# A four-layer graph network kernel: the value weights in one load, and layer 0's other loads issued some row tiles earlier

## The chip, the cores and the metric

The kernel runs on one core of a Trainium2 chip. A core has four computing engines that run side by side, each through its own instructions in order: TensorE (PE, matrix products; PEld is its loading of the stationary operand), VectorE (DVE), ScalarE (ACT) and GpSimd (POOL). SyncE (SP) only issues transfers. Sixteen DMA engines carry the transfers of all queues. The metric is device time in microseconds (us) of one launch; smaller is better.

## The reference

There are N = 2708 nodes with 512 features each (x) and an adjacency matrix adj (2708 x 2708) of which most entries are zero. Four layers follow each other; each normalises x over the features, applies a relu, computes something with adj, and adds it to x:

```python
# layer 0
h = relu(layernorm(x)); head = adj > 0, each row divided by its norm
x = x + ((adj + head) @ h) / rowsum(adj + head)
# layer 1: attention with 8 heads of 64, masked where adj is not one or more
x = x + sum over heads of softmax(q k^T / 8 - 1e16 * (1 - max(adj, I))) @ (h Wv) @ Wo
# layer 2
g = relu(adj @ (h W1) + b1); g = relu(adj @ (g W3) + b3); x = x + tanh(g Wf + bf)
# layer 3
x = x + ((adj != 0) @ (h W + b)) / degree
```

The mask of layer 1 is so strong that, if the largest entry of a row of adj stands alone and the scores are bounded, a row attends to one node only: the one where that row is largest. The kernel computes layer 1 in this way: it finds the place of each row's maximum (two passes of DVE over a row tile), multiplies by one product of the value and output weights, and gathers rows. Flags are collected on the way (that the scores are bounded, that no entry is negative, that the maximum is alone), and if a flag is set, a slow version of the layers runs instead.

## The kernel before, in words

Rows of adj are handled in NT = 22 tiles of 128 (the last has 20). Layer 0 is the part that the change touches; it takes the first 522 us of the span.

For each row tile, a slab of adj (128 x 2708, 1.35 MB) is loaded by SP (`load_slab`, L480) into one of three buffers named `ar`. On ACT, `row_norm` (L501) takes the signs of the slab (L510) and counts them (L515), and `row_sum` sums it (L529). `attended` (L535) finds the maximum and its place on DVE (L542, L544). Counted masks of three tiles go through TensorE (`count`, L273), ranks are formed, and `search` (L369) turns them on DVE into lists of the rows and blocks that aren't empty. POOL then gathers those (`gather_adj` L562 from adj, `gather_rows` L580 from h). The product of a row tile (L778) takes six dense blocks and five to eight gathered ones (the last tile: two gathered ones alone); for the first LEAD = 3 tiles it takes all 22 blocks. After it, `xt` is formed on DVE (L787) and normalised; `after` (L714) transposes the result on TensorE (L192), copies it on ACT (`hT`, L193) and multiplies it by the weights `wvo` of layer 1 (L158), whose result `yo` is stored.

The loop over m runs one row tile of products while the statistics of a tile up to eight further on are taken (`stats_to`, L677). Slabs 0, 3, 4, 5 and 1, 2 are needed early for their counts but their signs and maxima are not taken then: the tiles in `LATE` (3, 4, 5, 0, 1, 2) are loaded a second time, and `count_signs` (L493) and `attended` run on them in the last row tiles:

```python
if m + 8 > NT and late:
    if late[0] not in slab:
        load_slab(late[0])
    if len(late) > 1:
        load_slab(late[1])
    count_signs(late[0])
    attended(late.pop(0))
```

Weights come in between. At the very start ACT's queue loads the value weights, 1 MB in eight heads with runs of 256 bytes (`load_values`, L432), and the output weights (L436). `value_weights` (L438) transposes the first on TensorE (16 transposes, L445, four rounds of four with a copy by DVE, L446, after each), and multiplies the two into `wvo` (L158, copied by ACT, L450). `score_bound` (L453) loads the query and key weights (1 MB each, L461) and squares them on ACT (L464) at row tile 15. W1, 1 MB, is loaded and split into three parts for layer 2 (`load_w` L170, `split_w` L209, four rounds of ACT L197 and L207 and DVE L199 and L204) at row tile 17; W3 is loaded after it.

The order in which each engine gets its instructions is not just that of the program: the framework's scheduler moves an instruction ahead of others on its engine if its operands are free by the scheduler's own reckoning of times. To hold a transfer to its row tile, the kernel writes one element of its destination from that tile's `xt` with a small DVE copy (`behind`, L162, recorded under L164): the transfer then has to wait for it.

Of the kernel before, what the change touches and what calls it, by code (L numbers as in the profile page):

```python
# [9 lines left out]
FP = mybir.dt.float32  # L10
# [12 lines left out]
P = 128  # L23
# [19 lines left out]
def kernel(  # L43
# [27 lines left out]
    nc = tc.nc  # L71

    N, D = x.shape
    H, _, DK = wk_d.shape
    NT = (N + P - 1) // P
    NFULL = N // P
    TAIL = N - NFULL * P
    NCD = D // P
# [83 lines left out]
    def behind(dst, last):  # L162

        nc.vector.tensor_copy(dst, last)  # L164
# [41 lines left out]
        )  # L206
        nc.scalar.activation(lo, lo.bitcast(FP), AF.Copy, scale=-SHIFT)  # L207

    def split_w(pool, raw, tag):  # L209

        w = [pool.tile([P, NCD, D], FR, name=f"{tag}{i}") for i in range(3)]
        for c in range(NCD):
            split_b(*(part[:, c, :] for part in w), raw[:, c, :])
        return w

# [8 lines left out]
    with tc.tile_pool(name="l0_slab", bufs=2) as slabs, tc.tile_pool(  # L224
# [199 lines left out]
                norm(wp, h0[t], n, h0[t], AF.Relu)  # L424
                nc.gpsimd.dma_start(out=h0d[span(t)], in_=h0[t][:n])

        wv = wset.tile([P, NCD, D], FP, name="wa0")
        wo = wset.tile([P, NCD, D], FP, name="wa1")

        def load_values():  # L430
            for h in range(H):
                nc.scalar.dma_start(  # L432
                    out=wv[:, :, h * DK : (h + 1) * DK],
                    in_=wv_d[h].rearrange("(c p) k -> p c k", p=P),
                )
            nc.scalar.dma_start(out=wo, in_=wo_d.rearrange("(c p) k -> p c k", p=P))  # L436

        def value_weights():  # L438

            wvo = hp.tile([P, NCD, D], FP, name="wvo")  # L440
            wvt = wset.tile([P, NCD, D], FP, name="wa2")
            for r in range(NCD):
                pt = ps_tr.tile([P, NCD, P], FP, name="pt")
                for c in range(NCD):
                    nc.tensor.transpose(pt[:, c, :], wv[:, c, r * P : (r + 1) * P], ident)  # L445
                nc.vector.tensor_copy(wvt[:, r, :], pt.rearrange("p c k -> p (c k)"))  # L446
            for r in range(NCD):
                acc = ps_y.tile([P, D], FP, name="yacc")
                project(acc, wvt[:, :, r * P : (r + 1) * P], P, wo)
                nc.scalar.copy(wvo[:, r, :], acc)  # L450
            return wvo

        def score_bound(last):  # L453


            sq = hp.tile([P, 2], FP, name="sq")
            for i, src in enumerate((wq_d, wk_d)):
                wqk = wset.tile([P, NCD, D], FP, name=f"wa{i}")
                wqk = wqk.rearrange("p c k -> p (c k)")
                behind(wqk[:1, :1], last)  # L460
                nc.sync.dma_start(  # L461
                    out=wqk, in_=src.rearrange("h (a b) k -> (h a) (b k)", a=P // H)
                )
                nc.scalar.activation(wqk, wqk, AF.Square, accum_out=sq[:, i : i + 1])  # L464
            tot = ps_small.tile([P, P], FP, name="rb")
            nc.tensor.matmul(tot[:, :2], ones, sq, start=True, stop=True)
            nc.scalar.copy(sq, tot[:, :2])
            nc.vector.tensor_mul(sq[:, 0:1], sq[:, 0:1], sq[:, 1:2])
            limit = (SCORE_MAX * float(DK) ** 0.5 / D) ** 2
            over = bad[:1, BAD_BOUND : BAD_BOUND + 1]  # L470
            nc.vector.tensor_scalar(over, sq[:1, 0:1], limit, None, op0=ALU.is_lt)
            nc.vector.tensor_scalar(over, over, -1.0, 1.0, op0=ALU.mult, op1=ALU.add)
# [17 lines left out]
                bad[:n, BAD_NEG + m : BAD_NEG + m + 1], sum_sgn[:n], cnt[:n], ALU.not_equal  # L490
            )

        def count_signs(m):  # L493

            sgn = slabs.tile([P, N], BF, name="sgn", bufs=GROUP)
            cnt, sum_sgn = (wp.tile([P, 1], FP, name=name, bufs=4) for name in ("cnt", "sum_sgn"))
            nc.scalar.activation(sgn, slab[m], AF.Sign, accum_out=sum_sgn)
            nc.scalar.activation(sgn, sgn, AF.Relu, accum_out=cnt)
            flag_negative(m, sum_sgn, cnt)
# [156 lines left out]


        order_n = ZERO[:1] + FIRST + ZERO[1:] + list(range(LEAD + GROUP, NT))
        late = list(LATE)
        normed, near, far = [0], [LEAD], [LEAD]  # L660
        listable = set()

# [14 lines left out]
        def stats_to(m):  # L677


            while normed[0] <= order_n.index(m):  # L680
# [7 lines left out]
                if t == 0 or t % GROUP == GROUP - 1 or t >= NT - 2:  # L688
# [7 lines left out]
                        todo.extend(partial(search, k) for k in masks)  # L696
                        do_next(0)
                    masks.clear()
                if t in late:
                    slab.pop(t)  # L700
                else:
                    attended(t)
# [63 lines left out]
        for m in range(NT):  # L766
# [27 lines left out]
                do_next(2 if NT - 8 < m < NT - 5 else 1)  # L794
            stats_to(min(2 * m + 6, m + 8, NT - 1))
            gathers_to(m + 2)
            if m + 8 > NT and late:
                if late[0] not in slab:
                    load_slab(late[0])
                if len(late) > 1:  # L800
                    load_slab(late[1])
                count_signs(late[0])
                attended(late.pop(0))
            if m + 8 == NT + 1:
                todo.append(partial(rank_rows, list(range(1, LEAD))))
                todo.extend(partial(search, k) for k in range(1, LEAD))
            if m == NT // 2 + 4:
                score_bound(xt[:1, :1])
            if m == NT - LEAD - 1:
                for t in range(1, LEAD):  # L810
                    gather_adj(t)
            if m == NT // 2 + 6:
                wr = load_w(wset, w1_d, "wr", lambda w: behind(w[:1, 0, :1], xt[:1, :1]))
                w1 = split_w(wset, wr, "wa")
                wr = load_w(wset, w3_d, "wr")
        flush()
        degrees()
# [949 lines left out]
```

## Time and profile before

| | us |
|---|---|
| median of 3 runs | 1499.95 (1498.87 to 1506.9) |
| the profiled execution | 1489.76 |
| its span, first to last instruction | 1488.0 |
| PE busy | 1298.3 (87%) |
| DVE busy | 946.2 (64%) |
| ACT busy | 690.3 (46%) |
| POOL busy | 657.6 (44%) |
| layer 0's last product ends | 522.6 |

The profile is that of one execution. It gives for each instruction its engine, line, start and length, and for an idle stretch ahead of it what ended it; DMA transfers show as packets and as landings. Busy shares are means over the whole span, and stages with different limits are in them, so the tables of stretches below give them stage by stage. Instructions that issue transfers stand under the queue of their engine (ACTq, SPq). A wait put down to "remote" is one whose source the profile doesn't know; "issue" means that the engine waited for nothing that it shows. An fp32 matrix product is recorded as two matmuls, a transpose as one. The ends of matmuls are modelled.

### The profile page before, as it was taken

The numbers are of one execution on the slowest core, as the hardware profiler recorded it, in microseconds if no ns is written. First come the engines' busy times: TensorE is split into PE (matmuls) and PEld (weight loads), VectorE is DVE, ScalarE is ACT, GpSimd is POOL, SyncE is SP. The second block draws the span as 40 slices with busy tenths as digits, with TensorE's granted clock in tenths as the row PEclk, the third lists the DMA queues.
The fourth block names the chain that finished last, engine by engine and source line by source line (L and its number), as shares of the span: only waits on it lengthen the run. The fifth ranks groups of instructions, "written<-read, shape, count | busy, mean of one in ns | idle before, by whom it ended". The sixth has DMA issues, their size and how long they took to land.

```text
span 1488.0 us, 15510 instructions
## 1 busy us (share of the span) xinstructions
PE 1298.3 (87%) x4430; PEld 774.4 (52%) x4430; DVE 946.2 (64%) x1932; ACT 690.3 (46%) x1051; POOL 657.6 (44%) x673
## 2 busy tenths in 40 slices
PE   3987687878958849988999999899999999877997
PEld 1333233333423337745665666466666666555776
DVE  3685776869969769743343446365666656665686
ACT  5965543463256246432333334344445444554453
POOL 1254366565754432054544442244334335326652
PEclk9997789899989979999999999999999999988999
DMA  9977887978797498366777777756555666557885
GB/s 349 375 244 249 268 272 242 315 242 247 250 341 284 145 308 279 131 220 209 252 222 233 237 233 234 243 176 187 174 173 170 195 195 202 175 193 221 275 261 159
DMA packets 200056, 349.04 MB, mean 235 GB/s; under 512 B 26406, under 2 KB 113024, under 8 KB 196229
## 3 DMA queue, kind: packets, MB, share of 16 engines
q1 hardware_dynamic: 149177, 200.80, 40.7%
q0 software_dynamic: 46032, 145.05, 31.2%
q10 hardware_dynamic: 4752, 2.10, 0.6%
q8 instruction: 37, 0.61, 0.2%
q14 instruction: 58, 0.48, 0.1%
HBM read 284.58 MB, written 63.29 MB: 234 GB/s over the span
## 4 chain that ended last, share of the span: by engine, by line
PE 51%; issue 5%; DMA 3%; DVE 2%; another core or an unknown queue 2%; POOL 1%; ACT 1%; SPq 0%; DVEq 0%; ACTq 0%; POOLq 0%
PE aggs L987 14%; PE main L900 9%; PE agg L984 8%; PE mixed L900 4%; PE aggs L984 4%; PE pt L875 3%; PE agg L1171 2%; PE aggs L1171 2%; DMA raw<-in_adj_t_dram 1%; PE aggs L999 1%; PE agg L900 1%; PE pt L1171 1%; POOL wb L935 1%; PE mixed L1171 1%
## 5 line engine op out<-in xcount | busy, mean ns | idle before, releaser
L987 PE MATMUL aggs<-gg,ac 128*128 128x512 f32 (+1 forms) x520 | 232.3, 594 | 3.4 <-DMA gg<-g1d,idx_g 3.4
L935 POOL DMA_INDIRECT gg<-g2d,idx_g x130 | 131.1, 1008 | 220.2 <-PE aggs L987 170.7
L935 POOL DMA_INDIRECT gg<-g1d,idx_g x130 | 133.9, 1030 | 180.1 <-PE aggs L987 109.0
L778 PE MATMUL acc<-h,inc 128*128 128x512 f32 (+1 forms) x348 | 171.1, 632 | 19.6 <-DVE inc L630 14.1
L562 POOL DMA_INDIRECT ac<-in_adj_t_dram,idx_a x130 | 127.9, 984 | 133.4 <-DMA lst<-ac 62.3
L987 PEld LDWEIGHTS aggs<-gg,ac 128*128 128x128 f32 (+1 forms) x520 | 97.9, 189 | 110.6 <-issue 103.0
L580 POOL DMA_INDIRECT h<-h0d,idx_g x111 | 117.2, 1056 | 57.0 <-issue 28.7
L971 ACT ACTIVATE a_hi<-raw 128x384 fp32r<-128x384 f32 x84 | 43.6, 520 | 167.3 <-issue 92.2
L778 PEld LDWEIGHTS acc<-h,inc 128*128 128x128 f32 (+1 forms) x348 | 66.7, 201 | 99.0 <-issue 81.5
L984 PE MATMUL agg<-ghi,a_hi 128*128 128x512 f32 x252 | 114.8, 456 | 3.3 <-ACT a_hi L971 2.4
L158 PE MATMUL yacc<-wvo,hT 128*128 128x512 f32 (+1 forms) x176 | 91.0, 663 | 28.8 <-issue 23.3
L778 PE MATMUL acc<-h,incl 128*128 128x512 f32 (+1 forms) x222 | 102.3, 609 | 0.0
L984 PE MATMUL agg<-glo,a_lo 128*128 128x512 f32 x252 | 102.2, 405 | 0.0
L972 DVE TENSOR_TENSOR a_lo<-raw,a_hi 128x384 fp32r<-128x384 f32 x84 | 47.3, 563 | 85.3 <-ACT a_hi L971 51.0
L984 PE MATMUL aggs<-gs,a_s 128*128 128x512 f32 x252 | 100.3, 401 | 0.6 <-DVE gs L204 0.6
L935 POOL DMA_INDIRECT gg<-hidr,idx_h x65 | 68.5, 1053 | 51.1 <-issue 11.3
L881 DVE SCALAR_TENSOR_TENSOR v_lo<-pt,v_hi 128x512 fp32r<-128x512 f32 (+1 forms) x88 | 56.5, 664 | 41.8 <-ACT v_hi L880 23.4
L862 DVE SCALAR_TENSOR_TENSOR u<-aggs,u 128x512 f32<-128x512 f32 x42 | 28.9, 687 | 77.9 <-PE aggs L987 68.3
L158 PEld LDWEIGHTS yacc<-wvo,hT 128*128 128x128 f32 (+1 forms) x176 | 35.2, 209 | 77.4 <-issue 66.1
L778 PEld LDWEIGHTS acc<-h,incl 128*128 128x128 f32 (+1 forms) x222 | 42.9, 195 | 54.4 <-issue 53.0
L880 ACT ACTIVATE v_hi<-pt 128x512 fp32r<-128x512 f32 (+1 forms) x88 | 48.6, 578 | 45.6 <-PE pt L875 35.8
L542 DVE MAX8 top<-ar 128x8 f32<-128x2708 f32 (+1 forms) x22 | 65.4, 2971 | 0.0
(307 smaller groups left out, 2812.3 us busy)
## 6 DMA issues: line engine op xcount, KB each, us to landing
ar<-in_adj_dram SPq DMA_DIRECT2D x27, 1354.0 KB
raw<-in_adj_t_dram SPq DMA_DIRECT2D x122, 192.0 KB
slot<-x SPq DMA_DIRECT2D x41, 256.0 KB
at<-in_adj_t_dram SPq DMA_DIRECT2D x27, 384.0 KB
ranks<-rank_b SPq DMA_DIRECT2D x20, 485.0 KB
ac<-lst SPq DMA_DIRECT2D x16, 384.0 KB
h<-in_x_dram SPq DMA_DIRECT2D x21, 256.0 KB
h0d<-h POOLq DMA_DIRECT2D x21, 256.0 KB
```

The costliest lines, as they stand in the source:

```text
L158: nc.tensor.matmul(acc[:n], hT[:, c, :n], w[:, c, :], start=(c == 0), stop=(c == NCD - 1))
L542: nc.vector.max(top[:n], ar[:n])
L562: nc.gpsimd.indirect_dma_start(out=ac[:, c, :n], out_offset=None, in_=adj_units, in_offset=bass.IndirectOffsetOnAxis(ap=idx_a[:, m, c0 + c ...
L580: nc.gpsimd.indirect_dma_start(out=g, out_offset=None, in_=h0d[:, :], in_offset=bass.IndirectOffsetOnAxis(ap=idx_g[:, m, c : c + 1], axis=0),)
L778: nc.tensor.matmul(acc[:n], a, g, start=(i == 0), stop=(i == len(pairs) - 1))
L880: nc.scalar.activation(hi[d], pt[d], AF.Relu, scale=UP)
L881: nc.vector.scalar_tensor_tensor(lo[d], pt[d], 0.0, hi[d].bitcast(FP), op0=ALU.max, op1=ALU.subtract)
L900: nc.tensor.matmul(acc[:n], a[:, c, :n], b[:, c, :], start=first and c == 0, stop=last and c == NCD - 1,)
L935: nc.gpsimd.indirect_dma_start(out=gs[c], out_offset=None, in_=gd[:, :], in_offset=bass.IndirectOffsetOnAxis(ap=index[:, m, c : c + 1], ax ...
L984: nc.tensor.matmul(acc[:n], a[:k, i, :n], b[:k], start=st, stop=sp)
L987: nc.tensor.matmul(mixed[:n], a, g, start=(c == 0 and not dense_of(m)), stop=(c == len(chunks) - 1),)
L1171: nc.tensor.matmul(bank_h(m)[: rows(m)], a, b, start=(i == 1), stop=(i == total))
```

## The change

Four things are changed, all in layer 0.

1. The value weights come in one load, ordered so that a partition holds four neighbouring rows of each head, in runs of 1 KB. Because of the new order a head's 64 columns are no longer next to the following head's, and the 16 transposes of 128 x 128 become 32 products of a 128 x 64 block with the identity; DVE's copy after each round puts the elements back in order.
2. The score weights are loaded at row tile 11 (before: 15), and squared at row tile 13, with a `behind` on the target of the sums.
3. W1 is loaded at row tile 14 (before: 17) and split at row tile 16, with a `behind` on each of the four rounds; W3's load follows the split.
4. The first late slab is loaded at row tile 14 (before: 15), so that each is loaded one row tile ahead of its use; its signs are held to their row tile by a `behind` on the sign mask.

```diff
@@ -206,10 +206,12 @@
         )
         nc.scalar.activation(lo, lo.bitcast(FP), AF.Copy, scale=-SHIFT)
 
-    def split_w(pool, raw, tag):
+    def split_w(pool, raw, tag, first=None):
 
         w = [pool.tile([P, NCD, D], FR, name=f"{tag}{i}") for i in range(3)]
         for c in range(NCD):
+            if first:
+                first(w[0][:, c, :])
             split_b(*(part[:, c, :] for part in w), raw[:, c, :])
         return w
 
@@ -424,15 +426,15 @@
                 norm(wp, h0[t], n, h0[t], AF.Relu)
                 nc.gpsimd.dma_start(out=h0d[span(t)], in_=h0[t][:n])
 
-        wv = wset.tile([P, NCD, D], FP, name="wa0")
+
+        wv = wset.tile([P, H, NCD, DK], FP, name="wa0")
         wo = wset.tile([P, NCD, D], FP, name="wa1")
 
         def load_values():
-            for h in range(H):
-                nc.scalar.dma_start(
-                    out=wv[:, :, h * DK : (h + 1) * DK],
-                    in_=wv_d[h].rearrange("(c p) k -> p c k", p=P),
-                )
+            nc.scalar.dma_start(
+                out=wv.rearrange("p h c k -> p h (c k)"),
+                in_=wv_d.rearrange("h (p c) k -> p h (c k)", c=NCD),
+            )
             nc.scalar.dma_start(out=wo, in_=wo_d.rearrange("(c p) k -> p c k", p=P))
 
         def value_weights():
@@ -442,18 +444,21 @@
             for r in range(NCD):
                 pt = ps_tr.tile([P, NCD, P], FP, name="pt")
                 for c in range(NCD):
-                    nc.tensor.transpose(pt[:, c, :], wv[:, c, r * P : (r + 1) * P], ident)
-                nc.vector.tensor_copy(wvt[:, r, :], pt.rearrange("p c k -> p (c k)"))
+                    for k in range(0, P, DK):
+                        head = wv[:, (r * P + k) // DK, c, :]
+                        nc.tensor.matmul(
+                            pt[k : k + DK, c, :], head, ident, start=True, stop=True
+                        )
+                nc.vector.tensor_copy(wvt[:, r, :].rearrange("k (p c) -> k c p", c=NCD), pt)
             for r in range(NCD):
                 acc = ps_y.tile([P, D], FP, name="yacc")
                 project(acc, wvt[:, :, r * P : (r + 1) * P], P, wo)
                 nc.scalar.copy(wvo[:, r, :], acc)
             return wvo
 
-        def score_bound(last):
-
-
-            sq = hp.tile([P, 2], FP, name="sq")
+        scores = []
+
+        def load_scores(last):
             for i, src in enumerate((wq_d, wk_d)):
                 wqk = wset.tile([P, NCD, D], FP, name=f"wa{i}")
                 wqk = wqk.rearrange("p c k -> p (c k)")
@@ -461,6 +466,14 @@
                 nc.sync.dma_start(
                     out=wqk, in_=src.rearrange("h (a b) k -> (h a) (b k)", a=P // H)
                 )
+                scores.append(wqk)
+
+        def score_bound(last):
+
+
+            sq = hp.tile([P, 2], FP, name="sq")
+            for i, wqk in enumerate(scores):
+                behind(sq[:1, i : i + 1], last)
                 nc.scalar.activation(wqk, wqk, AF.Square, accum_out=sq[:, i : i + 1])
             tot = ps_small.tile([P, P], FP, name="rb")
             nc.tensor.matmul(tot[:, :2], ones, sq, start=True, stop=True)
@@ -490,10 +503,11 @@
                 bad[:n, BAD_NEG + m : BAD_NEG + m + 1], sum_sgn[:n], cnt[:n], ALU.not_equal
             )
 
-        def count_signs(m):
+        def count_signs(m, last):
 
             sgn = slabs.tile([P, N], BF, name="sgn", bufs=GROUP)
             cnt, sum_sgn = (wp.tile([P, 1], FP, name=name, bufs=4) for name in ("cnt", "sum_sgn"))
+            behind(sgn[:1, :1], last)
             nc.scalar.activation(sgn, slab[m], AF.Sign, accum_out=sum_sgn)
             nc.scalar.activation(sgn, sgn, AF.Relu, accum_out=cnt)
             flag_negative(m, sum_sgn, cnt)
@@ -656,7 +670,6 @@
 
 
         order_n = ZERO[:1] + FIRST + ZERO[1:] + list(range(LEAD + GROUP, NT))
-        late = list(LATE)
         normed, near, far = [0], [LEAD], [LEAD]
         listable = set()
 
@@ -696,7 +709,7 @@
                         todo.extend(partial(search, k) for k in masks)
                         do_next(0)
                     masks.clear()
-                if t in late:
+                if t in LATE:
                     slab.pop(t)
                 else:
                     attended(t)
@@ -794,24 +807,29 @@
                 do_next(2 if NT - 8 < m < NT - 5 else 1)
             stats_to(min(2 * m + 6, m + 8, NT - 1))
             gathers_to(m + 2)
-            if m + 8 > NT and late:
-                if late[0] not in slab:
-                    load_slab(late[0])
-                if len(late) > 1:
-                    load_slab(late[1])
-                count_signs(late[0])
-                attended(late.pop(0))
+
+            step = m - (NT - 8)
+            if 0 <= step < len(LATE):
+                load_slab(LATE[step])
+            if 0 < step <= len(LATE):
+                count_signs(LATE[step - 1], xt[:1, :1])
+                attended(LATE[step - 1])
             if m + 8 == NT + 1:
                 todo.append(partial(rank_rows, list(range(1, LEAD))))
                 todo.extend(partial(search, k) for k in range(1, LEAD))
-            if m == NT // 2 + 4:
+            if m == NT // 2:
+                load_scores(xt[:1, :1])
+            if m == NT // 2 + 2:
                 score_bound(xt[:1, :1])
             if m == NT - LEAD - 1:
                 for t in range(1, LEAD):
                     gather_adj(t)
-            if m == NT // 2 + 6:
+            if m == NT // 2 + 3:
                 wr = load_w(wset, w1_d, "wr", lambda w: behind(w[:1, 0, :1], xt[:1, :1]))
-                w1 = split_w(wset, wr, "wa")
+            if m == NT // 2 + 5:
+                w1 = split_w(
+                    wset, wr, "wa", lambda w: behind(w[:1, :1], xt[:1, :1])
+                )
                 wr = load_w(wset, w3_d, "wr")
         flush()
         degrees()
```

## The prediction, made before the changed kernel was seen

> **What bounds the kernel now.** I read first where the chain of waits begins. Its first piece starts at 518.28 us, so it says nothing about layer 0, where all of the change lies, and layer 0 has to be read by stages. The table of stretches (PE, PEld, DVE, ACT, POOL busy, then granted clock, DMA share and GB/s) cuts it up:
>
> ```profile
> 25.00:75.00 50.00, 41.08 (x104) 16.86 (x103) 33.37 (x124) 47.37 (x75) 11.97 (x22) 0.90 1.04 378
> 75.00:350.00 275.00, 217.18 (x556) 94.76 (x555) 200.94 (x433) 140.36 (x165) 152.34 (x154) 0.87 0.82 263
> 350.00:402.00 52.00, 50.56 (x151) 22.73 (x150) 50.78 (x115) 16.09 (x24) 34.48 (x34) 0.99 0.78 239
> 402.00:442.00 40.00, 26.99 (x67) 12.04 (x65) 28.57 (x42) 18.44 (x22) 26.37 (x22) 0.83 0.91 329
> 442.00:512.00 70.00, 59.80 (x149) 26.44 (x148) 66.49 (x124) 33.45 (x42) 30.31 (x32) 0.95 0.66 227
> ```
>
> At the start ACT (47.4 of 50) and the DMA engines (share 1.04) are full. From 350 to 402, PE and DVE are both full (50.6 and 50.8 of 52). Then comes a hole, 402 to 442, where DVE is busy 28.6 of 40 and PE 27.0, while the DMA share rises to 0.91; after it DVE is full again (66.5 of 70) to the end of the layer. The clock falls to 0.83 in the hole because PE stands still. So the tail is DVE's, with one gap in it. The timelines of ACT and PE (start, length, line, idle before it) show what made the gap:
>
> ```profile
> 413.68 0.56 ACT L722 COPY yo<-yacc 128x512 f32<-128x512 f32 x1
> 420.11 2.46 ACT L497 ACTIVATE sgn<-ar 128x2708 bf16<-128x2708 f32 x1 [5.86 <-issue]
> ...
> 428.33 1.91 ACT L464 ACTIVATE wa<-wa 128x2048 f32<-128x2048 f32 x1 [0.64 <-issue]
> ...
> 435.45 0.60 ACT L193 ACTIVATE hT<-pt 128x512 f32<-128x512 f32 x1 [5.11 <-remote]
> ```
> ```profile
> 422.49 0.60 PE L192 MATMUL pt<-ident,hn 128*128 128x128 f32 x4
> 436.10 4.64 PE L158 MATMUL yacc<-wvo,hT 128*128 128x512 f32 x6 [13.01 <-issue]
> ```
>
> PE has the transposes of row tile 15 done at 423.1 and needs ACT's copy (L193) to go on. ACT executes in order and had placed the signs of the late slabs (L497) and the square of the query weights (L464) ahead of that copy, though their loads were issued only at 410 to 413; it waits 5.9 us for the first slab and reaches the copy 12.4 us late. Of that, 5.1 us are a wait whose source the trace doesn't know. What DVE lost, in its list of waits from 402 to 512 (us, times, longest):
>
> ```profile
> DVE bad L489 <- ACT sgn L498: 4.8, 1, 4.8
> DVE end L376 <- DMA ar<-rank_l: 3.1, 1, 3.1
> DVE ar L540 <- issue: 2.6, 1, 2.6
> DVE wa L199 <- ACT wa L197: 1.5, 1, 1.5
> DVE end L376 <- DMA ranks<-rank_b: 1.1, 1, 1.1
> ```
>
> **The change part by part.** *Late slabs, score weights, W1 loaded ahead, uses held.* The first late slab is loaded at row tile 14 instead of 15, the two score weights at 11 instead of 15 with their squares at 13, W1 at 14 instead of 17 with its split at 16. Three of DVE's five waits have their cause removed: 4.8 (L489 behind the late signs), 2.6 (L540 waiting for the first late slab), 1.5 (the split waiting for W1's load) = 8.9 us. The waits on rank_l and rank_b stay, 4.2 us, but with a slab already there the maximum of a late slab (2.97 us a pass, two passes a slab) can stand in the first of them, so the upper end is 13.1. On PE the same stretch loses 13.0 here and 4.8 at 468 to 473, where the normalisation L186 sat behind a late sign (L497, 5.5 us idle); DVE can't follow a gain of 17.8, it has only 13.1 idle. I take 9.0 off the tail. The lower end is 0: the copy may merely find the next in-order instruction in front of it.
>
> *Added holds.* The changed lines issue one-element DVE copies: 4 for the scores (2 were there), 6 for the late signs, 5 for W1 (1 was there), 12 new ones at 0.13 us (the row of L164), 1.6 us, in a stretch where DVE is full; some fall in the gap. I take 1.0. Behind each hold on its engine waits all that follows: on ACT the transposes' copy of the next row tile if the late sign is put first, on SP every load after the score weights, which now waits for row tile 11 (before, SP waited 1.0 us at tile 15 for the same thing).
>
> *DMA moved.* 2.1 MB leave the full stretch 412 to 442 for 345 to 360, 2.4 MB (slab and W1) come forward to 395 to 410. At the 369 GB/s of 412 to 442 that is 5.7 and 6.5 us of all DMA engines. The share is 0.55 from 350 to 360 and 0.54 from 370 to 380, so 4.5 + 4.6 us are free there, which covers the first; from 390 to 410 it is 0.86 and 0.73, 4.1 free, which leaves 2.4 of the second uncovered. PE at 97% there is fed by gathers issued one row tile ahead. I take 0, up to 12.2 if neither is covered.
>
> *Value weights.* ACT's queue spends 8.62 us issuing eight loads and starts computing at 10.33 (timelines of ACT and DVE):
>
> ```profile
> 0.75 8.62 ACTq L432 DMA_DIRECT2D wa<-in_L_gnn_Wvs_dram  x8
> 10.33 1.28 ACT L510 ACT_TABLE_LOAD   x1 [10.33 <-DMA wa<-in_L_gnn_Wvs_dram]
> 22.74 0.69 DVE L446 COPY wa<-pt 128x512 f32<-128x512 f32 x1 [3.25 <-PE pt L445]
> ```
>
> One issue ends at about 1.5. Slab 0's last packet lands at 6.4, so the first sign can start at 6.5 and not 11.6: 5.1 us sooner. But ACT's next wait, 5.3 us up to 23.5, is for DVE's count, which stands behind the third copy of the transposed weights at 22.74; ACT's early start is worth something only if that copy is not later. The DMA itself gets cheaper: ACT's queue moved 2.10 MB in 41.5% of the first 20 us, 8.3 us of all engines; at the 356 GB/s of the first 60 us it would be 5.9, so at most 2.4 are saved, in a stretch that is DMA-bound. Against it, 16 transposes become 32 ordinary fp32 products. In the rows, four transposes of 128 columns take 0.60 us; eight records (four products) of 512 columns take 3.60, so one of 128 columns is 0.225, or 0.45 at half clock. 32 of them are 7.2 to 14.4 us against 2.4 to 4.3: 4.8 to 10.1 more, in four rounds that each wait for DVE's copy. PE is idle 17.6 of the first 25 us, which hides the work but not the chain: three of the four rounds stand ahead of the count, 3.6 to 7.6 us. The first round must now wait for the whole load and not for its first two heads (9.04 us before); at 356 GB/s one load of 1.05 MB behind slab 0 lands at 9.4, and the first copy stood at 16.9 behind DVE's statistics of the fourth tile of x, which hides that. The four copies now write with a stride; no row here shows such a write, so 0.69 each to twice that, 2.8 us in all; I take the row they are nearest to, their own, and 0. Between a gain of 5.1 + 2.4 = 7.5 and a loss of 7.6 + 2.8 = 10.4 I take -1.0: of the DMA saving a part, since ACT is as full as the DMA engines there, and the other two nearly cancel.
>
> The Trainium skill, TensorE: Matmul & The Clock Gate (Terms, xbus), speaks against this step: it says that transpose mode is four times as fast for fp32. The rows above give a factor near 1.5 for whole groups (0.60 against 0.90). By the rule's factor one product would be 0.60 and 32 of them 19.2 us, 12 more than by the rows, and the start would lose where I let it break even. The same skill, DMA: Bandwidth & Descriptors (Issuing engines are not separate DMA queues), holds that sequencer time for issues is usually small; here the row has 8.62 us for eight, so the measurement decides, and by the rule the early start would be worth nothing.
>
> **Sum.** -9.0 + 1.0 + 0 - 1.0 = -9.0 us. The profiled execution took 1489.76 us (span 1488.0), 0.7% under the median of 1499.95; 9 us off give 1480.8 there and **1491.0** against the median. All of the gain happens before 522; from there the path (last y stored, gathered, 16.5 us of PE idle to 539) is untouched.
>
> **The rivals.** *No change, 1498 (from 1493 to 1503).* DVE is the bound from 350 to 512 and gets 1.6 us more work. If the order of instructions that follows from the new dependencies puts another wait in the hole (the unexplained 5.1 us, or DVE's scan of 5.8 us ahead of the next row tile), only 2.6 + 1.5 of the 8.9 come back and the copies eat half: -2. For it: DVE is 95% busy after 442. Against it: the hole is 11 us of idle DVE whose named causes are removed.
>
> *Slower, 1508.* The mechanism is the DMA at row tiles 11 and 14: gathers that arrive late behind 2.1 and 2.4 MB. PE and DVE have no slack from 350 to 402, so each microsecond of a late gather is a microsecond of the end. Price 5.7 + 6.5 = 12.2, less 4.1 that stays of the tail: +8. It decides from the point where over half of the bursts isn't covered. For it: one gather of POOL, at 402.00, took 6.48 us where the others take 0.95, in this very stretch. Against it: the free share of 350 to 380.
>
> *The change doesn't do what it says.* The order of instructions on each engine is made by a scheduler with its own idea of times; one that already put signs 10 us ahead of their loads could put held signs ahead of the next copy, too. Then it is 1498 to 1503, and I count it with no change.
>
> **How the numbers follow.** About 0.5% (7.5 us) is what a measurement of this kernel can tell from no change. Faster by more, the forecast, 0.52: its own range goes from 1492 down to 13.1 in the tail and 7.5 at the start, both in full, 1479. Within 0.5%, 0.30. Slower by more, 0.18. The range for all, 1479 to 1508, reaches from there to the price of the slower rival, and leaves out what lies beyond it, where the start loses as well.
>
> **What would show it.** In the changed profile: the DVE waits on L498, L540 and the split gone, PE's gap of 13 us at tile 15 under 3, DVE over 85% busy in the 40 us before the late signs end, the transposed copy (L193) within 1 us of its transposes, last product of layer 0 at about 513 instead of 522; squares on ACT near 385 with no wait. At the start, ACT's first sign at 6.5 to 7. Wrong is the forecast if the gap only moves, if DVE's idle time from 350 to 512 stays above 10 us, or if ACT's second wait ends after 27 instead of 23.5. Wrong on the other side: PE idle over 3 us between 345 and 410.

## The result, and the profile after

The changed kernel takes 1500.39 us (median of 19 runs, 1478.84 to 1516.10), the one before 1501.75 us in 19 runs beside it. The ratio is 0.9978 with a 95% interval from 0.9954 to 1.0002: no difference that can be told from none, where I had forecast 9 us less. Measured again with 12 runs against 29 (e13 below) it is 1.0020 (0.9986 to 1.0053). A ratio leaves disturbed runs out and a median doesn't, so the two need not agree to the last us.

The table of stretches of the changed kernel, cut at the same times as the one of before (PE, PEld, DVE, ACT, POOL busy, then granted clock, DMA share, GB/s):

```profile
25.00:75.00 50.00, 42.42 (x128) 17.58 (x124) 32.97 (x117) 45.87 (x74) 11.92 (x22) 0.97 1.01 356
75.00:350.00 275.00, 207.13 (x552) 90.56 (x550) 197.50 (x423) 140.51 (x163) 147.53 (x148) 0.89 0.78 256
350.00:402.00 52.00, 46.29 (x129) 20.28 (x130) 43.11 (x104) 18.86 (x27) 29.23 (x30) 0.91 0.93 305
402.00:442.00 40.00, 34.35 (x90) 15.65 (x88) 37.23 (x68) 10.23 (x15) 29.58 (x26) 0.96 0.85 280
442.00:512.00 70.00, 61.97 (x153) 27.18 (x154) 65.89 (x129) 37.52 (x47) 40.39 (x36) 0.98 0.71 247
```

The hole from 402 to 442 is filled: DVE 37.2 of 40 instead of 28.6. But the stretch ahead of it, 350 to 402, was full and now isn't: DVE 43.1 of 52 instead of 50.8, while the DMA share rose from 0.78 to 0.93. DVE's idle time in the three stretches together was 1.2 + 11.4 + 3.5 = 16.2 us and is 8.9 + 2.8 + 4.1 = 15.8. The gap moved.

At row tile 15, PE and ACT, by their timelines:

```profile
439.96 0.60 PE L192 MATMUL pt<-ident,hn 128*128 128x128 f32 x4
442.73 3.70 PE L158 MATMUL yacc<-wvo,hT 128*128 128x512 f32 x8 [1.09 <-issue]
```
```profile
442.08 0.60 ACT L193 ACTIVATE hT<-pt 128x512 f32<-128x512 f32 x1 [7.63 <-PE rb L633]
```

The copy that was 12.4 us late comes 1.5 us after its transposes, and PE's 13.0 us are gone. Of DVE's waits from 402 to 512 the three of 4.8, 2.6 and 1.5 us have shrunk to 1.1, 1.1 and nothing (its list of waits):

```profile
DVE incl L636 <- PE rb L633: 2.0, 1, 2.0
DVE ar L340 <- DMA ar<-cnt_b: 1.2, 1, 1.2
DVE bad L502 <- ACT sgn L512: 1.1, 1, 1.1
DVE ar L554 <- ACT sgn L511: 1.1, 1, 1.1
```

From `xt` of row tile 15 to the last product of layer 0 the kernel before took 112.2 us and the changed one 101.8. It starts that stretch later, though: `xt` of row tile 0 stands at 86.7 instead of 81.9, and row tiles 11 to 15 take 75.5 instead of 65.6. The last product ends at 526.1, not at 522.6 as before or at 513 as I had said. (What follows, the same code in both, took 974.0 us here and 965.4 in the profile of before; in e13, e14 and e15 below it takes 982.9, 974.8 and 974.0.) In the stretch that lost time stands a wait of a kind that the trace of before has, too (ACT's and PE's timelines):

```profile
353.66 0.60 ACT L193 ACTIVATE hT<-pt 128x512 f32<-128x512 f32 x1 [9.38 <-remote]
```
```profile
344.45 0.60 PE L192 MATMUL pt<-ident,hn 128*128 128x128 f32 x4
354.31 2.07 PE L158 MATMUL yacc<-wvo,hT 128*128 128x512 f32 x2 [5.40 <-issue]
```

PE's transposes are recorded as done at 345.05 and ACT had nothing else to do; still its copy began 8.6 us later. What ends that wait the trace doesn't know. A second profile of the same kernel (e13 below) takes 75.6 us for row tiles 11 to 15, with other waits of this kind there (ACT's copy of `yo`, 7.8 and 6.0 us).

One load is not where the change was meant to put it. The first late slab is to be loaded at row tile 14, but its load isn't held, and in the changed profile SP issues it 18.7 us after `xt` of row tile 11, behind the score weights (issued at 361.95 and 364.33); the kernel before issues it, with the second, just ahead of `xt` of row tile 15. It is the 23rd load of a slab in both, the first after the slab of 20 rows (SP's timelines, before and after):

```profile
410.01 0.89 SPq L485 DMA_DIRECT2D ar<-in_adj_dram  x2
```
```profile
367.45 0.33 SPq L498 DMA_DIRECT2D ar<-in_adj_dram  x1
```

The same holds for every kernel below that has part 4 of the change: the load stands 11 to 28 us after `xt` of row tile 11. So 3.5 MB come into that stretch, the score weights' 2.1 and this slab's 1.4.

### The profile page after: what moved, and what is told of

It reads as the page before. It is cut to its first block, busy times and chain, and to the rows that moved or that the text cites. A ratio compares the mean times of both kernels' runs of the same rounds, so it can differ in the third digit from the quotient of the medians.

```text
span 1500.1 us, 15607 instructions
## 1 busy us (share of the span) xinstructions
PE 1302.3 (87%) x4478; PEld 774.2 (52%) x4478; DVE 946.5 (63%) x1944; ACT 689.7 (46%) x1051; POOL 663.9 (44%) x673
## 3 DMA queue, kind: packets, MB, share of 16 engines
q10 hardware_dynamic: 1568, 2.10, 0.4%
## 5 line engine op out<-in xcount | busy, mean ns | idle before, releaser
L576 POOL DMA_INDIRECT ac<-in_adj_t_dram,idx_a x130 | 137.5, 1058 | 132.9 <-DMA lst<-ac 58.9
L791 PE MATMUL acc<-h,inc 128*128 128x512 f32 (+1 forms) x348 | 163.2, 610 | 12.4 <-DVE inc L644 7.9
L158 PE MATMUL yacc<-wvo,hT 128*128 128x512 f32 (+1 forms) x176 | 97.6, 705 | 54.1 <-ACT hT L193 40.5
L594 POOL DMA_INDIRECT h<-h0d,idx_g x111 | 111.8, 1008 | 54.0 <-issue 28.0
L990 DVE TENSOR_TENSOR a_lo<-raw,a_hi 128x384 fp32r<-128x384 f32 x84 | 47.2, 562 | 80.4 <-ACT a_hi L989 44.6
L953 POOL DMA_INDIRECT gg<-hidr,idx_h x65 | 72.0, 1108 | 51.6 <-issue 13.5
L524 ACT ACTIVATE sgn<-ar 128x2708 bf16<-128x2708 f32 (+1 forms) x22 | 54.0, 2455 | 25.2 <-DMA ar<-in_adj_dram 22.9
```

Of the source, the lines that this page charges most:

```text
L158: nc.tensor.matmul(acc[:n], hT[:, c, :n], w[:, c, :], start=(c == 0), stop=(c == NCD - 1))
L524: nc.scalar.activation(sgn[:n], ar[:n], AF.Sign, accum_out=sum_sgn[:n])
L576: nc.gpsimd.indirect_dma_start(out=ac[:, c, :n], out_offset=None, in_=adj_units, in_offset=bass.IndirectOffsetOnAxis(ap=idx_a[:, m, c0 + c ...
L594: nc.gpsimd.indirect_dma_start(out=g, out_offset=None, in_=h0d[:, :], in_offset=bass.IndirectOffsetOnAxis(ap=idx_g[:, m, c : c + 1], axis=0),)
L791: nc.tensor.matmul(acc[:n], a, g, start=(i == 0), stop=(i == len(pairs) - 1))
L953: nc.gpsimd.indirect_dma_start(out=gs[c], out_offset=None, in_=gd[:, :], in_offset=bass.IndirectOffsetOnAxis(ap=index[:, m, c : c + 1], ax ...
```

## The experiments

Most of them are cut behind layer 0, where all of the change lies: y is copied to the output after the last row tile, and all that follows is left out. Up to there the cut kernel before and the cut changed kernel have the whole ones' order of instructions on PE, DVE, ACT and POOL. For a cut kernel the ratio is to the whole kernel before, run beside it. "Stretch" times are read from the `xt` (L787) of row tiles in each profile: start to tile 0, 0 to 11, 11 to 15, and 15 to the last product. A profile is one execution, and its time can lie up to 7 us from its kernel's median (e7), so a difference of a few us between two of them is weak evidence.

The theories: **bursts** (the moved loads delay what the full stretch needs), **bound chain** (the moved squares and their product do), **start** or **products** (the value weights' step costs what I took as nil), **order** (the scheduler lays the whole layer out anew once a step at its start changes), **lost later** (behind layer 0).

**e1, e5, e16: the kernel before, cut.**

```diff
-    gp = short.enter_context(tc.tile_pool(name="g", bufs=1))
-    ...
+    nc.sync.dma_start(out=out, in_=y)
```

> The kernel before, cut off after layer 0: everything behind the last row tile's y is left out and y itself is copied to the output, so its time is layer 0 plus one copy that is the same in every such cut. It is the base of the next three. The whole kernel's last product of layer 0 ended at 522.6 us; with the store, the copy of 5.5 MB at some 180 to 370 GB/s and the start and end of the program I expect 550 to 580 us. All theories agree on it.

> The cut kernel before once more, as the base for the next three on the same chip, and as a second sample of its profile: if the chip is the one of the first cuts, 489 to 501 us; if it is like the one of the whole kernels' profiles, some 545 us, with waits of 5 to 17 us between PE's transposes and ACT's copy (L193) that no engine of the profile ends. The waits at row tile 15 (PE idle 8.5 us there in the first cut) should come back, since the order of instructions is the same.

> The cut kernel before a third time, as base. On the chip of e1 and e5 (whole kernel before 1416 us): 489 to 500. On the one of e9 to e12 (1491): 545 to 556, with over 100 us of DVE's idle time in layer 0 against 66 to 74, at the same order of instructions.

Measured: 494.69 us (ratio 0.3471, 0.3452 to 0.3491), 494.84 (0.3479, 0.3461 to 0.3496) and 556.33. The kernels ran on different chips, and the same program takes 12% longer in layer 0 on some: on the chips of e1 to e8, e17 and e18 the whole kernel before takes 1416 to 1421 us, on those of e9 to e16 and of the first result 1491 to 1502. The tables of stretches of e1 and of e16, both from 83 us, about where row tile 0 ends in both:

```profile
83.00:302.00 219.00, 198.02 (x532) 87.84 (x531) 193.87 (x418) 135.79 (x158) 148.33 (x147) 0.94 0.92 308
```
```profile
83.00:302.00 219.00, 169.13 (x434) 73.82 (x432) 162.83 (x347) 105.59 (x124) 121.30 (x125) 0.88 0.79 260
```

All engines do less per us in e16, and the DMA engines too (0.79 against 0.92): nothing is full. e16's lists of waits from 83 to 345 have entries that e1's have nowhere:

```profile
ACT yo L722 <- remote: 20.0, 2, 12.1
...
ACT hT L193 <- remote: 9.1, 1, 9.1
```
```profile
PE rb L619 <- remote: 10.1, 2, 6.1
```

No profile of e1 to e8, e17 and e18 has a wait put down to "remote" in layer 0, and every profile from the other chips has some. So I compare kernels on chips of the same kind only, and call them the quick and the slow ones.

**e2, e13: the changed kernel, cut and whole.**

> The changed kernel, cut off in the same way. Beside the cut kernel before: my forecast, -9.0 us. Theory 'given back inside layer 0' (the tail's gain is real, but the start and row tiles 11 to 15 return it): 0, within 4. Theory 'lost later' (layer 0 is shorter by the forecast, and the layers behind it, whose code is the same, lose it): -7 to -10.

> The changed kernel whole, once more, against the kernel before. Theory 'given back inside layer 0': ratio 0.997 to 1.002, as in the cuts (-0.4 us of 494.7) and the first result (0.9978). My forecast: 0.994. Theory 'lost later': last product of layer 0 some 8 us earlier than before's, and the rest 8 us longer.

Measured: cut 494.26 us (0.3488, 0.3473 to 0.3503), level with e1 and e5 by the median, 1 to 2 us over them by the ratio, within the intervals; whole 1503.91 against 1496.85, ratio 1.0020 (0.9986 to 1.0053). "Given back inside layer 0" holds, on both kinds of chip: cut and whole agree within their intervals, so nothing needs to be lost later. Stretches of e2 against e1: 85.7 against 83.6, then 210.7 against 218.1, 69.5 against 64.3, and 101.4 against 107.6.

**e3, e17, e8: the value weights.** e3 and e17 are the kernel before with part 1 of the change alone, cut and whole. e8 has the one load, but the old transposes and plain copies:

```diff
-                    nc.tensor.transpose(pt[:, c, :], wv[:, c, r * P : (r + 1) * P], ident)
+                    nc.tensor.transpose(
+                        pt[:, c, :], flat[:, c * D + r * P : c * D + (r + 1) * P], ident
+                    )
```

> The kernel before with the value weights' step alone (one load, products in place of transposes, strided copies), cut after layer 0. My forecast for this step: -1.0 us. Theory 'start' (the step costs what the profile shows up to row tile 0, 4.8 us later): +4 to +5. Theory 'bursts' (the loss sits in the moved loads): within 2 of 0. Theory 'order' (the scheduler lays out all of layer 0 anew once a step at its start changes; waits that nothing in the change explains come and go): any sign, up to 10, with PE's gaps at other row tiles than before.

> The whole kernel before with the value weights' step alone. My forecast for the step: -1.0 us. Theory 'products' (32 products, each round's strided copy 0.36 us longer, and a first round that waits for the whole load): +2 to +4, ratio 1.001 to 1.003, row tile 0 at 86, 3 to 4 us later than before. Rival: the 2 us that e2 and e3 had back between row tiles 0 and 11 make it 0.

> The kernel before with the value weights' one load, but with the 16 transposes and plain copies of before on what it loads, so that the combined weight has its columns in another order and the values that come out of it are others. It takes the products and the strided copies away and keeps the early start and the landing of the load. Forecast for a load that gains all of the 5.1 + 2.4 us: -7. Theory 'landing' (the first round waits for the whole load, 15.8 us, and gains nothing): 0, row tile 0 at 82 to 84. Theory 'products' (the loss is in the 32 products and strided copies): -2 to -4, row tile 0 near 80, 5 us before the changed kernel's.

Measured: e3 497.74 us (0.3513, 0.3495 to 0.3530), over e1 and e5 by 3 us in the median and 5 by the ratio; e17 1426.71 against 1420.58, ratio 1.0026 (0.9996 to 1.0057), 3.7 us; e8 494.67 (0.3498, 0.3486 to 0.3510), level by the median and 3 us over by the ratio. The step costs some 3 us where I had -1.0, though e17 alone doesn't exclude nil. The profile of e3, PE and DVE:

```profile
15.97 1.97 PE L446 MATMUL pt<-ident,wa 128*64 128x128 f32 x16 [15.97 <-DMA wa<-in_L_gnn_Wvs_dram]
```
```profile
17.98 1.05 DVE L449 COPY wa<-pt 128x512 f32<-128x512 f32 x1 [5.61 <-PE pt L446]
```

The one load lands at 16.0, not at 9.4: in e3's trace its packets move from 3.0 to 15.3, among those of four tiles of x (to 11.1) and of a second slab of adj (to 14.8). A round of eight products takes 1.97 (1.09 at full clock) against 1.08 (0.60) for four transposes; a strided copy takes 1.05 against 0.69. In e8 ACT begins its second sign at 23.4, in e5 at 26.6, in e3 at 25.5: the one load gains 3.2 us there, products and copies take 2.1 back. Row tile 0 stands at 83.6 in e8, and at 85.7 to 86.7 in all five profiles with the products, against 80.4 to 83.6 in all fourteen with the old step: 86.2 against 81.9 on average. So the early start of ACT gains nothing at row tile 0.

By its own forecast e8 came out as "landing" had it: level, with row tile 0 between 82 and 84. "Order" came true as well: e3 and e8 have the same order of instructions on PE, ACT and POOL, and both differ from e5 on PE, DVE and ACT up to the end of layer 0. So e3 against e8 shows the products and strided copies alone: 2.5 us at row tile 0, and 3 us in the median or 2 by the ratio, on two chips. e8 against e5, on one chip, shows the load and the new order together: 0 or 3 us, not clear of noise.

Where in layer 0 the step's 3 us end up the profiles don't show. On the quick chips those with the products reach row tile 11 at 296.3 to 297.0 us (e2, e3, e17), those with the old step at 296.7 on average (292.6 to 301.7): what row tile 0 lost is given back by then, as e17's rival had it. On the slow chips it isn't (348.8 and 352.6 against 340.2 to 347.5).

**e4, e9, e14: the other three parts.** The changed kernel with the value weights as before, cut twice, and whole.

> The kernel before with the other three parts alone (late slabs, score weights, W1 ahead, uses held), the value weights as before, cut after layer 0. My forecast for these parts: -8.0 us. Theory 'bursts' (2.1 MB at row tile 11 and 2.4 MB at 14 delay the gathers): 0 to +4, with row tiles 11 to 15 taking 75 us as in the changed kernel instead of 65.6. Theory 'start': -8 to -10, row tiles 11 to 15 near 66. Theory 'order': like the forecast only if PE's gaps stay where they were up to row tile 11.

> e4 once more (three parts without the value weights), as the base of the next two, whose order of instructions is nearly its own. Both theories: as before within 3 us of e4's standing to the kernel before, row tiles 11 to 15 in 67 to 69 us, DVE waiting 3 to 4 us for the loaded ranks (L378) near row tile 13.

> The whole kernel with the late slabs, score weights and W1 ahead and the holds, but with the value weights as before. From the cuts (e4 2 us under e1, e3 3 us over it): -2 us, ratio 0.998 to 0.999, and 1 to 3 us under the whole changed kernel. By my forecast of the parts: -8. If cuts don't stand for the whole, anything from -10 to +5.

Measured: e4 492.70 us (0.3471, 0.3452 to 0.3490); e9 551.20 on a slow chip (0.3663, 0.3644 to 0.3681); e14 1494.44 against 1496.85, ratio 0.9980 (0.9950 to 1.0010). The forecast of -8.0 for these parts falls. e4 has the tail's gain (102.1 against 107.6 in e1 and 109.9 in e5), and row tiles 11 to 15 take 68.4 against 64.3 and 63.0. Two waits stand there (timelines of DVE and PE in e4):

```profile
331.21 0.15 DVE L378 TENSOR_SCALAR end<-ranks 128x1 f32<-128x1 f16 x1 [3.53 <-DMA ranks<-rank_b]
```
```profile
342.29 0.58 PE L476 MATMUL rb<-sq,ones 128*128 128x2 f32 x2 [4.12 <-ACT wa L474]
```

PE stands before the product of the squares, with the transposes of row tile 13 queued behind it. The ranks don't stand behind the score weights: the last packet of those moves at 309.6, and the ranks' load is issued at 326.47. It is late because their store is (322.82, 30.2 us after `xt` of row tile 11; 28.1 in e1 and e5), and the store stands in SP's queue behind a load that waits for a store of x to land (SP's list of waits in e4, 293 to 328):

```profile
SPq L740 <- DMA x<-xt: 5.2, 1, 5.2
```

**e6: bound late.**

```diff
-            if m == NT // 2 + 2:
+            if m == NT // 2 + 4:
                 score_bound(xt[:1, :1])
-            if m == NT // 2 + 5:
+            if m == NT // 2 + 6:
                 w1 = split_w(
```

> The three parts without the value weights (as in e4), but the squares of the score weights and their product at row tile 15 instead of 13 and W1's split at 17 instead of 16; all loads stay where e4 has them. In e4 row tiles 11 to 15 took 68.5 us against 64.3. Theory 'bursts' (the 2.1 MB at tile 11 and 2.4 MB at 14 delay the gathers): they still take 68 or more, total as e4, 0 to -2 against before. Theory 'bound chain' (PE reached the product of the squares, L476, 4.1 us before ACT had both squares, and the transposes of row tile 13 stood behind it): 64 to 65 there, total 3 to 4 less than e4's, -5 against before.

Measured: 496.68 us (0.3503, 0.3489 to 0.3516); row tiles 11 to 15 take 67.2, so in this pair of profiles the bound chain is worth 1.2 of e4's excess, and the tail, with the squares and W1's split later, takes 4.5 more (106.6).

**e7: late slabs alone.**

> The kernel before with the late slabs alone one row tile ahead and their signs held; score weights, W1 and value weights as before. By my forecast the tail's gain of 9.0 is mostly this part's (4.8 + 2.6 of the 8.9 us): -6. Both theories on the give-back: row tiles 11 to 15 as before, near 64, so -5 to -6 in all; if instead the score weights and W1, still loaded at 15 and 17, keep ACT or DVE waiting, 0 to -2.

Measured: 504.41 us (0.3557, 0.3542 to 0.3571), 10 us slower than before: the clearest effect of all, and against my -6. Row tiles 11 to 15 are as before (63.9), and the tail takes 113.1; the profile is of the quickest of its runs (497.78), so it shows a part only. ACT in e7:

```profile
414.46 2.19 ACT L197 ACTIVATE wa<-wr 128x512 fp32r<-128x512 f32 x4 [6.25 <-DMA wr<-in_L_gnn_W_dram]
416.56 0.57 ACT L193 ACTIVATE hT<-pt 128x512 f32<-128x512 f32 x1
```

With the signs held, the scheduler put W1's split (no hold, load as late as before) ahead of the transposes' copy, and ACT waits 6.2 us for W1, and PE 5.9 us for ACT. The wait changed its name. So the slabs alone don't bring the tail's gain, and the three parts together do; which of the other two they need was not tried.

**e10, e11: the dose of the score loads.** e4 without them (the squares are taken of other weights), and e4 with each loaded twice; e18 is e10 whole.

```diff
-            if m == NT // 2:
-                load_scores(xt[:1, :1])
```

> e4 without the 2.1 MB of score weights: the squares are taken of the value and output weights that already lie in the same buffers, so the bound is one over other numbers; squares, holds, product and all else stay, and PE, ACT and POOL run the same instructions in the same order. Theory 'bursts': row tiles 11 to 15 back to 63 to 65 us from 68.5, DVE's wait for the ranks near tile 13 gone, -3 to -5 against e9. Theory 'bound chain' (the squares and the product behind them are what delays row tile 13): 67 to 69 as in e9, 0 to -1.

> e4 with each of the two score weights loaded twice into the same buffer, 2.1 MB more at row tile 11. Theory 'bursts': another 4 to 6 us in row tiles 11 to 15 (72 to 75) and in all. Theory 'bound chain': the squares wait for the second load if it lands after 338 us, else 0.

> e14 without the loads of the score weights: the squares are taken of the value and output weights that lie in the same buffers, so only the number that is compared with the bound is another one. Theory 'bursts': 3 to 7 us under e14, ratio to before 0.993 to 0.996. Theory that the moved loads are covered, as the prediction had it: as e14, 0.998.

Measured: e10 542.64 us (0.3615, 0.3597 to 0.3633), e11 545.37 (0.3628, 0.3612 to 0.3643), both below e9's 551.20; e18 1419.52 against 1420.58, ratio 0.9988 (0.9967 to 1.0009). Row tiles 11 to 15: 68.5 in e10 and 66.4 in e18 without the loads; 71.1, 68.4 and 69.0 in e9, e4 and e14 with them; 76.0 in e11 with twice as much. By these profiles the first 2.1 MB cost 0.5 to 2.6 us in the stretch and the second 5 to 7, but others spread as much: on the slow chips kernels without score loads there take 65.6 to 70.5 (before, e16, e10, e12, e15), the changed kernel with a single dose 75.5 and 75.6, and on its own chip e18 takes no more than e17 (66.8), which moves none of these loads. In e11 DVE waits 5.7 us there for the ranks, in e9 never over 1 us, but in e12, without score loads in that stretch, 3.8. In the total the dose doesn't show: e9's profile has one of the unexplained waits in its tail (the copy at row tile 15 begins 15.1 us after its transposes), which e11's hasn't. e18 stays level with before, where "bursts" had 3 to 7 us less than e14. So "bursts" explains a part of the loss at most.

**e12, e15: the score weights elsewhere.** e12, cut, loads them at row tile 16, squares at 18 and splits W1 at 20. e15, whole, loads them at row tile 20 into freed slabs and squares them there.

> The three parts without the value weights, but with the score weights loaded at row tile 16 and squared at 18 instead of 11 and 13, and W1 split at 20 instead of 16, so that the 2.1 MB fall into the stretch whose DMA share was 0.65 in the first cut. Theory 'bursts': row tiles 11 to 15 in 63 to 65 us with the tail's gain kept, last product 460 us, -5 to -7 against the kernel before. Rival: in the tail the squares (3.8 us) and the split's eight passes stand ahead of the transposes' copies on ACT and in DVE's full stretch, and the gain turns into their wait: 0 to +3.

> As e14, but the score weights are loaded at row tile 20 into the buffers that the last slabs leave free, and squared there without holds, so that W1's buffers don't wait for them either. Theory 'bursts': row tiles 11 to 15 without the 4 to 5 us of e4, and the tail without the squares' wait of before: -6 to -8 us, ratio 0.995. Rival: two squares of 1.9 us on ACT stand between the signs and the copies of the last row tiles, and their product on PE waits for the load: 0 to -2, or slower when the last y is late for the next layer's gathers.

Measured: e12 554.40 us (0.3705, 0.3686 to 0.3724), over e9 by 3 us in the median and 6 by the ratio; e15 1507.33 against 1496.85, ratio 1.0044 (1.0008 to 1.0080). Neither is a way out, and row tiles 11 to 15 take 68.7 and 70.5, not the 63 to 66 of "bursts". In e12 the rival came true: the tail takes 111.4, and PE stands 6.6 us before the product of the squares. e15's tail takes 117.0, for another reason (DVE, ACT and PE):

```profile
444.48 0.75 DVE L794 SCALAR_TENSOR_TENSOR xt<-acc,deg,xt 128x512 f32<-128x512 f32 x1 [16.14 <-remote]
```
```profile
446.65 0.60 ACT L193 ACTIVATE hT<-pt 128x512 f32<-128x512 f32 x1 [23.89 <-remote]
```
```profile
447.30 5.49 PE L158 MATMUL yacc<-wvo,hT 128*128 128x512 f32 x6 [18.20 <-issue]
```

DVE, ACT and PE all stand for 16 us or more after products that PE is recorded to have finished at 427.6.

## Why the prediction was wrong, by its own steps

**Tail, -9.0: right in its mechanism, some 2 us too large.** On the quick chips row tile 15 to the last product takes 102.9 us on average with the squares at row tile 13 (e2, e4, e18), and 109.8 in the kernel before and the value step's variants (e1, e3, e5, e8, e17): -6.9. Over all profiles of these two kinds, nine and seven, it is -6.7. The named waits went as told. What I had wrong is whose gain it was: I put 7.4 of the 8.9 us to the late slabs, and alone they cost 10 (e7).

**DMA moved, 0: the first step that failed.** I said that the free share of 350 to 380 covers the score weights and that 2.4 us of the rest stay. On the quick chips row tiles 11 to 15 take 64.7 us on average without these parts (e1, e3, e5, e8, e17) and 68.4 with them (e2, e4, e6): +3.7. Two things were wrong. The first late slab came there too, 3.5 MB in all and not 2.1. And the DMA time that I took as free wasn't: over the 30 us from `xt` of row tile 11 the DMA share is 0.83 to 0.89 in those five profiles and 1.00 to 1.03 in those three (e5, then e4):

```profile
297.60:327.60 30.00, 29.91 (x88) 13.17 (x88) 30.00 (x69) 12.27 (x17) 22.98 (x24) 0.96 0.88 262
292.60:322.60 30.00, 28.62 (x88) 12.52 (x87) 30.00 (x68) 12.26 (x17) 19.91 (x21) 1.00 1.03 361
```

The slab alone costs nothing there in e7's profile (63.9, at a share of 0.94). In e2, e4 and e6 SP stands 4.7 to 8.5 us for a store of x to land, with the store of the ranks behind it; the ranks' load is issued 33.7 to 34.4 us after `xt` of row tile 11, in the five others 30.2 to 32.2, and DVE waits 2.8 to 3.7 us for it instead of 1.6 at most. The rest is PE's order (e4 waits 4.1 us before the product of the squares). That the full DMA engines make the store of x late fits these shares, but no run shows it apart. On the slow chips this chain isn't there (DVE waits for ranks 1.0 us at most in the first changed profile, e9, e13 and e14): the first pair's +9.8 has the 8.6 us of unexplained wait at its head, e13's 75.6 has others, and what of it the moved loads cost stays open.

**Value weights, -1.0: the second step that failed.** It measured +3 and +3.7 (e3, e17; e17's interval still holds nil). The bounds held, the value between them didn't: the load was taken to land at 9.4 and landed at 16.0, and the copies, taken at their old 0.69, take 1.05. The products were priced too high, not too low: a round of eight at 1.80 us (3.6 at half clock) where it takes 1.09 (1.97). Beside 0.60 (1.08) for a round of four transposes, one product costs no more than one transpose (0.14 and 0.15 us at full clock); there are twice as many. The rule of the Trainium skill that I had weighed (TensorE: Matmul & The Clock Gate, Terms) says four times for fp32; these rows don't show it. ACT's early start came as told (first sign at 7.13 instead of 11.63), but ACT then stands until 18.95 for DVE and until 23.41 for PE's count, where before it stood until 23.52 for DVE: its second sign begins at 25.37 instead of 26.27, and of 4.5 us 0.9 are left.

**Added holds, +1.0:** not tried alone.

The sum with what was measured on the quick chips: -6.9 + 3.7 + 3.7 = +0.5 us, the holds inside these. The cut changed kernel stands there at -0.4 us by the median and +2.4 by the ratio (e2 against e1), the whole one on the slow chips at -3.3 (0.9978) and +3.0 (1.0020). Of the rivals "no change" came true in number and half in its mechanism: the wait didn't return in the hole but ahead of it and at the start. I had named that place under "slower", and its sign, PE idle over 3 us between 345 and 410, is there (5.4).

One piece of evidence for that rival was misread. The gather of 6.48 us at 402.00 has nothing to do with DMA. POOL and DVE in the profile of before:

```profile
402.00 6.48 POOL L580 DMA_INDIRECT h<-h0d,idx_g  x1 [0.30 <-issue]
```
```profile
401.93 5.78 DVE L339 TENSOR_TENSOR_SCAN ar<-ar 1x2708 f16<-1x2708 f16 x1
```

and in the changed one:

```profile
419.16 5.36 POOL L576 DMA_INDIRECT ac<-in_adj_t_dram,idx_a  x1 [0.31 <-issue]
```
```profile
418.00 5.77 DVE L341 TENSOR_TENSOR_SCAN ar<-ar 1x2708 f16<-1x2708 f16 x1
```

POOL's issue of a gather lasts until DVE's scan has ended, 408.5 against 407.7 and 424.5 against 423.8, where others take 0.95. The Trainium skill, GPSIMD Engine Reference (Key points), says that the two share their interfaces to SBUF and that an instruction of DVE with two inputs there contends; the scan is one. It costs no time here: in the profile of before, the last gather of each of row tiles 11 to 16 is issued 30 us or more before its `xt`.

**What stays open:** the source of the waits of 5 to 19 us after PE's recorded ends. The order of instructions alone doesn't fix them, since e9 and e14 have the same and at row tile 15 the copy lags by 15.1 us in one and by nothing in the other; nor does the change make them, since the kernel before has them too. But they aren't random: in the first changed profile and in e13, the same kernel, ACT stands 17.4 and 17.0 us before the copy of row tile 0, 17.7 and 16.9 before that of row tile 5, and DVE 12.3 and 12.3 before `xt` of row tile 6. On the chips that have these waits layer 0 is 40 to 66 us longer, and one more or less is as much as the whole effect of the change. Where the value step's 3 us end up stays open, too.

No version beats both kernels: the best, e14, is at 0.9980 with 1 inside the interval.

## What to carry to other kernels

A hole in the profile is worth what it costs only if what is moved out of it lands where something is idle: ask for each moved instruction and load what then stands behind it in its own queue (a store of ranks behind a load that waits for a landing, transposes behind a product that waits for ACT), not only whether the DMA engines have time on average. Look in the trace, too, whether a load starts where the program has it: one that nothing holds may be issued row tiles earlier, as the late slab was. A wait that is taken away alone can hand its place to the next unheld instruction, as e7 shows; try the parts apart. Cut the kernel behind the stage that changes, and read several profiles before believing 9 us in one.

## What the runs showed of the hardware that I had not expected

- The same program took 494 us on some chips and 556 on others, with the difference between row tiles 0 and 11 (216 to 218 against 262).
- The changed load of 1 MB has 1 KB runs and 1568 packets in ACT's queue instead of 4752, and it still landed 6.6 us later than my estimate from 356 GB/s, in a stretch where other loads were under way.
- DVE's scan holds up POOL's issue of gathers for its whole 5.8 us.
